# Storing the last tile's second sample by transfers of 5, 121 and 2 partitions

## The chip, the cores and the metric

The kernel runs on one core of a Trainium2 chip. A core has a matrix engine (TensorE, PE), a vector engine (VectorE, DVE), an activation engine (ScalarE, ACT), a general engine (GpSimd, POOL) and SyncE (SP), which here only issues transfers. Sixteen DMA engines move data between the on-chip memory (SBUF, 128 partitions) and the device memory (HBM). The metric is the device time of one execution in microseconds, and lower is better.

## The reference, cut to what matters

For 1024 samples, each with 39 fields of 16 numbers in `xi` and `xj`, every pair of fields (r, c) with c < r gives an outer product of 16 x 16. There are 741 pairs. Each pair is normalised over all samples and elements, scaled and shifted by `gamma` and `beta`, and multiplied by a 16 x 16 weight.

```python
cross = xj[:, rows, :, None] * xi[:, cols, None, :]          # (1024, 741, 16, 16)
mean = jnp.mean(cross, axis=(0, 2, 3), keepdims=True)
var = jnp.mean(jnp.square(cross - mean), axis=(0, 2, 3), keepdims=True)
normed = (cross - mean) * jax.lax.rsqrt(var + BN_EPS)
normed = normed * gamma[None, :, None, None] + beta[None, :, None, None]
out = normed[:, :, None, :, :] * W[None, None, :, :, :]
return jnp.transpose(out, (0, 2, 1, 3, 4))                   # (1024, 1, 741, 16, 16) float32
```

The output is 1024 x 741 x 256 float32 numbers, 777 million bytes; the inputs are about 6 million.

## The kernel before

Partition p holds samples 8p to 8p + 7 (`NT` = 8). The statistics come first, from sums of the inputs. Then the output is made tile by tile. A tile is one row r of the pair triangle for `T` = 2 samples of every partition, so it holds 128 x 2 x r pairs. The order of tiles ends with r = 21 and then r = 17, for the samples 6 and 7 of each partition.

```python
T = 2
...
tiles = [(mid, t0, t0 // T * half // 2) for t0 in range(0, NT, T)]      # mid = 19
slot = 0
for r in (mid + 1, *range(F - 1, mid + 1, -1)):
    for t0 in range(0, NT, T):
        tiles.append((r, t0, slot * half))
        if r < F - 1:
            tiles.append((F - 1 - r, t0, slot * half + T * r))
        slot ^= 1
...
out_v = out.rearrange("(p t) o n i j -> p t (o n i j)", t=NT)
```

ScalarE and GpSimd make the products of a tile, VectorE (with a share for GpSimd) adds the shift and multiplies by the weight, and the tile is stored from SBUF. All stores are issued by SyncE, in the order of the tiles. The function that issues them:

```python
def store(n, c0, c1, t_from=0, t_to=T):
    r, t0, _ = tiles[n]
    n0 = first[r]

    whole = n >= len(FIRST_PIECES)
    step = 1 if r > mid and (whole or c1 == r) else t_to - t_from
    for t in range(t_from, t_to, step):
        if whole and step == 1 and t == t_to - 1:
            if c1 < r:
                continue
            c0 = 0
        nc.sync.dma_start(
            out_v[:, t0 + t : t0 + t + step, (n0 + c0) * EE : (n0 + c1) * EE],
            view(n)[:, t : t + step, c0:c1, :].rearrange("p t n e -> p t (n e)"),
        )
```

For the last tile r = 17 is below `mid`, so `step` is 2: one transfer takes both samples of all 128 partitions. It is issued once the last of these has run:

```python
def finish(n):
    ...
    size = 1 if n == RAW else T
    for t in range(0, T, size):
        for c0, c1 in zip(bounds(n), bounds(n)[1:]):
            for c in [*range(c0, min(c1, p0)), *range(max(c0, p1), c1)]:
                stt(
                    y[:, t : t + size, c, :],
                    y[:, t : t + size, c, :],
                    t_sb[:, n0 + c : n0 + c + 1],
                    w_dve.to_broadcast([P, size, EE]),
                    ALU.add,
                    ALU.mult,
                )
            store(n, c0, c1, t, t + size)
```

Of the kernel before, what the change touches and what calls it, by code (L numbers as in the profile page):

```python
# [14 lines left out]
T = 2  # L15
# [25 lines left out]
def tile_pair_outer_batchnorm(  # L41
# [15 lines left out]
    nc = tc.nc  # L57
    P = nc.NUM_PARTITIONS
    NB, F, E = xi.shape
    NT = NB // P  # L60
    EE = E * E
# [7 lines left out]
    tiles = [(mid, t0, t0 // T * half // 2) for t0 in range(0, NT, T)]  # L69
# [25 lines left out]
    out_v = out.rearrange("(p t) o n i j -> p t (o n i j)", t=NT)  # L95
# [41 lines left out]
    def view(n):  # L137
        r, _, u = tiles[n]
        return y_sb[:, u : u + T * r, :].rearrange("p (t n) e -> p t n e", t=T)
# [65 lines left out]
    def store(n, c0, c1, t_from=0, t_to=T):  # L205
        r, t0, _ = tiles[n]
        n0 = first[r]

        whole = n >= len(FIRST_PIECES)
        step = 1 if r > mid and (whole or c1 == r) else t_to - t_from  # L210
# [9 lines that stand above are left out]
# [14 lines left out]
    def weigh(n):  # L234

        y = view(n)
        for c0, c1 in zip(bounds(n), bounds(n)[1:]):
            affine(n, range(c0, min(c1, OWN)), (nc.vector,))
            nc.vector.tensor_tensor(  # L239
                y[:, :, c0:c1, :],  # L240
                y[:, :, c0:c1, :],
                w_dve.unsqueeze(1).to_broadcast([P, T, c1 - c0, EE]),
                ALU.mult,
            )
            store(n, c0, c1)
# [8 lines left out]
    def finish(n):  # L254
# [33 lines left out]
# [12 lines that stand above are left out]
# [262 lines left out]
```

## Time and profile before

| what | value |
|---|---|
| time, median of 3 | 1879.16 us (1879.11 to 1879.3) |
| span of the profiled execution | 1877.4 us |
| written to HBM | 776.99 MB |
| rate over the span, read and written | 417 GB/s |
| transfers that store output | 279, all issued by SyncE |

The span is the time from the first to the last instruction in one profiled execution. The page divides it into 40 slices of 46.9 us each; the last store falls into the last slice alone, so what happens in it has to be asked for with narrower windows. A DMA share of 1 means that all 16 DMA engines move data; one engine is 0.06.

### The profile page before, as it was taken

To read this page: it belongs to the slowest core of one execution; us is meant where nothing else is said; L and a number is where in the kernel's file an instruction comes from. 1 tells how busy PE (TensorE), PEld (TensorE's weight loads), DVE (VectorE), ACT (ScalarE), POOL (GpSimd) and SP (SyncE) were. 2 spreads that over 40 slices of the span, in tenths; PEclk is the share of its full clock that TensorE was granted. 3 is DMA by queue.
4 is the path that set the end of the run, shared out by engine and by line. 5 is a ranking of instruction groups with operands and counts; after the bars stand their busy time and mean duration, and the time that the engine had idled before them with its cause. 6 is when DMAs were issued, how large, how long until landed. Compare 5 with 4: busy or idle time off the path is not lost.

```text
span 1877.4 us, 9638 instructions
## 1 busy us (share of the span) xinstructions
PE 26.0 (1%) x130; PEld 23.3 (1%) x130; DVE 1723.9 (92%) x2640; ACT 1645.7 (88%) x3416; POOL 1532.4 (82%) x1746
## 2 busy tenths in 40 slices
PE   4000000000000000000000000000000000000000
PEld 4000000000000000000000000000000000000000
DVE  8999888899999999999999999999999999999994
ACT  8999888888888899989999999998999998989892
POOL 8999778787777788888888888888888888888882
DMA  5999999999999999999999999999999999999998
GB/s 199 385 421 424 411 421 422 428 427 424 428 427 425 428 426 425 427 425 427 419 425 432 425 425 432 424 432 424 431 426 430 425 432 425 430 428 426 428 430 350
DMA packets 53690, 783.63 MB, mean 417 GB/s; under 512 B 4720, under 2 KB 6384, under 8 KB 17008
## 3 DMA queue, kind: packets, MB, share of 16 engines
q1 hardware_dynamic: 52320, 779.72, 97.9%
q10 hardware_dynamic: 1296, 3.29, 0.5%
q14 instruction: 73, 0.60, 0.1%
q8 instruction: 1, 0.02, 0.0%
HBM read 6.00 MB, written 776.99 MB: 417 GB/s over the span
## 4 chain that ended last, share of the span: by engine, by line
DMA 56%; ACT 21%; DVE 17%; issue 3%; POOL 1%; SPq 0%; ACTq 0%; DVEq 0%; PE 0%; POOLq 0%
DMA out_dram<-y_sb 56%; ACT y_sb L147 20%; DVE y_sb L291 16%; POOL y_sb L149 1%; DVE y_sb L358 1%; ACT y_sb L230 0%; DVE y_sb L332 0%; POOL xs L169 0%; SPq L216 0%; DMA xi_sb<-in_r_xi_dram 0%; POOL y_sb L277 0%; POOL y_sb L342 0%; DVE y_sb L192 0%; DVE xs L182 0%; ACT y_sb L353 0%
## 5 line engine op out<-in xcount | busy, mean ns | idle before, releaser
L291 DVE SCALAR_TENSOR_TENSOR y_sb<-y_sb,st_sb,w_dve 128x512 f32<-128x512 f32 (+1 forms) x2511 | 1653.2, 738 | 117.2 <-issue 103.9
L147 ACT ACTIVATE y_sb<-xs,xj_sb 128x288 f32<-128x288 f32 (+20 forms) x3194 | 1514.8, 565 | 181.5 <-DMA out_dram<-y_sb 149.6
L149 POOL TENSOR_SCALAR y_sb<-xs,xj_sb 128x480 f32<-128x480 f32 (+27 forms) x1126 | 604.8, 561 | 14.2 <-DMA out_dram<-y_sb 14.1
L280 POOL TENSOR_TENSOR y_sb<-y_sb,w_sb 128x2048 f32<-128x2048 f32 (+3 forms) x155 | 517.7, 3346 | 87.4 <-ACT y_sb L275 77.8
L169 POOL TENSOR_TENSOR xs<-xi_sb,st_sb 128x640 f32<-128x640 f32 (+33 forms) x135 | 183.9, 1363 | 199.9 <-ACT y_sb L147 196.1
L277 POOL TENSOR_SCALAR y_sb<-y_sb,st_sb 128x512 f32<-128x512 f32 x291 | 196.8, 692 | 5.1 <-ACT y_sb L147 5.1
L275 ACT ACTIVATE y_sb<-y_sb,st_sb 128x512 f32<-128x512 f32 x160 | 100.2, 708 | 3.8 <-POOL y_sb L149 2.2
L192 DVE TENSOR_TENSOR y_sb<-xs,ps 128x256 f32<-128x256 f32 (+3 forms) x32 | 24.8, 817 | 0.5
L489 PE MATMUL ps<-y_sb 39*128 39x38 f32 (+37 forms) x76 | 16.4, 397 | 2.8 <-DVE y_sb L475 2.8
L489 PEld LDWEIGHTS ps<-y_sb 39*128 39x128 f32 x76 | 16.3, 329 | 3.1 <-DVE y_sb L475 3.1
L353 ACT ACTIVATE y_sb<-y_sb 128x1248 f32<-128x1248 f32 x8 | 9.9, 1244 | 2.8 <-POOL y_sb L342 2.7
L358 DVE TENSOR_REDUCE y_sb<-y_sb 128x78 f32<-128x1248 f32 x8 | 11.2, 1445 | 0.4 <-ACT y_sb L353 0.4
L147 ACT ACTIVATE y_sb<-xi_sb,xj_sb 128x304 f32<-128x304 f32 x24 | 11.4, 537 | 0.0
L342 POOL TENSOR_TENSOR y_sb<-xi_sb,y_sb 128x1248 f32<-128x1248 f32 x4 | 9.2, 2322 | 2.2 <-ACT y_sb L391 2.2
L239 DVE TENSOR_TENSOR y_sb<-y_sb,w_dve 128x2048 f32<-128x2048 f32 (+4 forms) x6 | 10.7, 1838 | 0.1
L332 DVE TENSOR_REDUCE y_sb<-xi_sb 128x39 f32<-128x624 f32 (+1 forms) x6 | 6.1, 1011 | 3.9 <-DMA xi_sb<-in_r_xi_dram 3.9
L342 POOL TENSOR_TENSOR y_sb<-xj_sb,y_sb 128x1248 f32<-128x1248 f32 x4 | 9.2, 2318 | 0.0
L378 PE MATMUL ps<-y_sb 128*39 128x79 f32 x48 | 8.0, 340 | 15.2 <-DVE y_sb L358 15.1
L232 POOL TENSOR_SCALAR y_sb<-y_sb,st_sb 128x512 f32<-128x512 f32 x8 | 6.4, 812 | 2.2 <-ACT y_sb L147 2.2
L230 ACT ACTIVATE y_sb<-y_sb,st_sb 128x512 f32<-128x512 f32 x9 | 6.5, 803 | 0.2 <-ACT y_sb L147 0.2
L332 DVE TENSOR_REDUCE y_sb<-xj_sb 128x39 f32<-128x624 f32 (+1 forms) x6 | 6.1, 1014 | 0.5 <-DMA xj_sb<-in_r_xj_dram 0.5
L378 PEld LDWEIGHTS ps<-y_sb 128*39 128x39 f32 x48 | 5.8, 177 | 17.2 <-DVE y_sb L358 10.6
(59 smaller groups left out, 37.3 us busy)
## 6 DMA issues: line engine op xcount, KB each, us to landing
out_dram<-y_sb SPq DMA_DIRECT2D x25, 2304.0 KB, 10.4
out_dram<-y_sb SPq DMA_DIRECT2D x12, 3840.0 KB, 21.7
out_dram<-y_sb SPq DMA_DIRECT2D x21, 2048.0 KB, 12.4
out_dram<-y_sb SPq DMA_DIRECT2D x12, 3584.0 KB, 23.1
out_dram<-y_sb SPq DMA_DIRECT2D x12, 3328.0 KB, 24.4
out_dram<-y_sb SPq DMA_DIRECT2D x12, 3072.0 KB, 25.2
out_dram<-y_sb SPq DMA_DIRECT2D x16, 2176.0 KB, 11.0
out_dram<-y_sb SPq DMA_DIRECT2D x8, 4352.0 KB, 24.1
```

The lines of the kernel that those rows point to most:

```text
L147: nc.scalar.activation(y, src, AF.Copy, scale=scale)
L149: engine.tensor_scalar(y, src, scale, 1.0, ALU.mult, ALU.mult)
L169: nc.gpsimd.tensor_tensor(xs, xi_sb[:, t0 : t0 + T, 0:r, :], s_sb[:, :, n0 : n0 + r, :].to_broadcast([P, T, r, E]), ALU.mult,)
L192: nc.vector.tensor_tensor(view(n)[:, t].rearrange("p n (i j) -> p n i j", j=E), xs[:, t].unsqueeze(2).to_broadcast([P, r, E, E]), xj_short ...
L275: nc.scalar.activation(y[:, :, c, :], y[:, :, c, :], AF.Identity, bias=t_c)
L277: nc.gpsimd.tensor_scalar(y[:, :, c, :], y[:, :, c, :], t_c, 1.0, ALU.add, ALU.mult)
L280: nc.gpsimd.tensor_tensor(y[:, :, c0:c1, :], y[:, :, c0:c1, :], w_sb.unsqueeze(1).to_broadcast([P, T, c1 - c0, EE]), ALU.mult,)
L291: stt(y[:, t : t + size, c, :], y[:, t : t + size, c, :], t_sb[:, n0 + c : n0 + c + 1], w_dve.to_broadcast([P, size, EE]), ALU.add, ALU.mult,)
L342: nc.gpsimd.tensor_tensor(devs[n % 7], sources[x][:, t0 : t0 + T], shift[:, x : x + 1, :].unsqueeze(3).to_broadcast([P, T, F, E]), ALU.sub ...
L358: nc.vector.tensor_reduce(to[:, t0 : t0 + T, F : 2 * F], devs[n % 7], AX.X, ALU.add)
L378: nc.tensor.matmul(ps_g[acc][0:F, 0 : 2 * F + 1], lhs, fb[:, t], start=t == 0, stop=t == NT - 1)
L489: nc.tensor.matmul(ps[:, :, first[r] - n0 : first[r] - n0 + r], pick[:, r, :], stq[:, :, 0:r], start=True, stop=True,)
```

## The change

For the last tile alone, and only where both samples would be stored at once, the store is split. The first sample goes as one transfer of 128 partitions through SyncE's queue, as any other store. The second sample goes as three transfers: partitions 121 to 125 and then 0 to 120 through GpSimd's queue, and partitions 126 and 127 through SyncE's queue. The bytes are the same, and so is everything computed. The aim is to give the 16 DMA engines different amounts of the last data: [...]

```diff
     def store(n, c0, c1, t_from=0, t_to=T):
         r, t0, _ = tiles[n]
         n0 = first[r]
+        if n == len(tiles) - 1 and t_to - t_from == T:
+
+            store(n, c0, c1, 0, T - 1)
+            for engine, p0, p1 in ((nc.gpsimd, 121, 126), (nc.gpsimd, 0, 121), (nc.sync, 126, P)):
+                engine.dma_start(
+                    out_v[p0:p1, t0 + T - 1, (n0 + c0) * EE : (n0 + c1) * EE],
+                    view(n)[p0:p1, T - 1, c0:c1, :].rearrange("p n e -> p (n e)"),
+                )
+            return
 
         whole = n >= len(FIRST_PIECES)
         step = 1 if r > mid and (whole or c1 == r) else t_to - t_from
```

## The prediction

> **What bounds the kernel now.** I read the page's busy times first, then its slices and its list of DMA queues, and then asked the trace for the last 40 us, because only the last store is edited.
>
> ```profile
> PE 26.0 (1%) x130; PEld 23.3 (1%) x130; DVE 1723.9 (92%) x2640; ACT 1645.7 (88%) x3416; POOL 1532.4 (82%) x1746
> ...
> DMA  5999999999999999999999999999999999999998
> GB/s 199 385 421 424 411 421 422 428 427 424 428 427 425 428 426 425 427 425 427 419 425 432 425 425 432 424 432 424 431 426 430 425 432 425 430 428 426 428 430 350
> ...
> q1 hardware_dynamic: 52320, 779.72, 97.9%
> ...
> q14 instruction: 73, 0.60, 0.1%
> ```
>
> The 16 DMA engines are at 90% or more in every slice but the first and the last, at 411 to 432 GB/s. The 759 MB of output set the time and the compute engines run beside them. Two things matter for this change: the last slice is not full (350 GB/s), and a second queue, "instruction", moves 0.60 MB in 73 packets beside the stores.
>
> The timeline of the end shows when the last tile is finished and its one store issued:
>
> ```profile
> 1845.63 4.69 DVE L291 SCALAR_TENSOR_TENSOR y_sb<-y_sb,st_sb,w_dve 128x512 f32<-128x512 f32 x7
> 1850.47 0.38 SPq L216 DMA_DIRECT2D out_dram<-y_sb  x1
> ```
>
> The list of issues for the stretch from 1845 us gives that store's size and its time to landing:
>
> ```profile
> out_dram<-y_sb SPq DMA_DIRECT2D x1, 4352.0 KB, 26.0
> ```
>
> So computing is over at 1850.3, and 26 us pass until the store has landed, at about 1876.5. The chain of waits (SyncE's) ends on this: "SPq L557 <- DMA out_dram<-y_sb" holds 25.4 us in 4 waits. Nothing but DMA can shorten those 26 us. The table by stretches cuts them up (columns: stretch, its length, busy time of PE, PEld, DVE, ACT, POOL, clock, DMA share of the 16 engines, GB/s):
>
> ```profile
> 1850.50:1867.80 17.30, 0.00 (x0) 0.00 (x0) 0.00 (x0) 0.00 (x0) 0.00 (x0) 1.00 0.98 419
> 1868.20:1870.15 1.95, 0.00 (x0) 0.00 (x0) 0.00 (x0) 0.00 (x0) 0.00 (x0) 1.00 0.25 107
> 1870.15:1872.10 1.95, 0.00 (x0) 0.00 (x0) 0.00 (x0) 0.00 (x0) 0.00 (x0) 1.00 0.19 80
> 1872.10:1873.40 1.30, 0.00 (x0) 0.00 (x0) 0.00 (x0) 0.00 (x0) 0.00 (x0) 1.00 0.13 54
> 1873.40:1876.05 2.65, 0.00 (x0) 0.00 (x0) 0.00 (x0) 0.00 (x0) 0.00 (x0) 1.00 0.06 26
> 1876.05:1877.40 1.35, 0.00 (x0) 0.00 (x0) 0.00 (x0) 0.00 (x0) 0.00 (x0) 1.00 0.00 0
> ```
>
> The shares are 4, 3, 2 and 1 sixteenths (0.25, 0.19, 0.13, 0.06). Twelve engines run dry together at about 1868.1. Four go on: one to about 1870.15, one to 1872.1, one to 1873.4 and one to 1876.05. Then 1.35 us of program end. The slowest engine alone costs 7.95 us of the span.
>
> Why those four? Every store has 128 rows, 8 for each engine, so the stores are even. Their lags are 2.05, 4.0, 5.3 and 7.95 us, together 19.3. One engine moves 26 to 27 GB/s (107/4, 80/3, 26/1), so this is 19.3 x 27 = 0.52 MB. The instruction queue moves 0.60 MB (0.57 MB after the first 100 us). [...]
>
> [...]
>
> **The change part by part.** Bytes do not change. One row of one sample is 17 x 256 x 4 = 17,408 bytes, and 17,408 / 26.8 GB/s = 0.65 us of one engine.
> 1. Removed: the one transfer of 128 x 2 rows, 16 rows per engine. Added: a transfer of the first sample, 8 rows per engine, in SyncE's queue as before. It only shortens the packet list; no effect on the end.
> 2. The second sample, before 8 rows on each engine: now 1 row on five engines, 11 on eleven, and 2 more rows on the two lowest. A relieved engine does 7 rows less: 7 x 0.65 = 4.55 us. A loaded one does 3 more: 1.95 us. An engine with one of the two SyncE rows gains only 6 x 0.65 = 3.9 us.
> 3. Issue costs: two issues on GpSimd and one more on SyncE (0.38 us for the one shown). GpSimd ends its arithmetic at about 1844 and waits for VectorE until 1850.3; the engines have 17 us of queued work from there. [...]
> [...] Then the eleven end at 1868.1 + 1.95 = 1870.05. The four end at 1870.15, 1872.1, 1873.4 and 1876.05 minus 4.55: 1865.6, 1867.55, 1868.85, 1871.5; one on the two lowest engines ends 0.65 later. The last end is 1871.5, or 1872.15[...]. The gain is 4.55 or 3.9 us: 1879.16 - 4.55 = 1874.6, or 1875.3. I take the smaller gain[...].
>
> **Rivals.**
> - All 16 engines are used by the 121 rows[...]: fifteen engines keep 8 rows, five get 1 more, two another. The slowest engine then has 9 or 10 rows in place of 8: +0.65 to +1.3 us, so 1879.8 to 1880.5. Against it: the odd numbers 5 and 121 would be pointless. In the profile nothing decides.
> - [...] the slowest engine is one of the eleven and gets 3 more rows, +1.95 us: 1881.1. Again only the plan of the change speaks against it.
> - GpSimd's queue is slow to start or its rows are cut into small packets, so the eleven loaded engines end late. They have 1.5 us in hand (1870.05 against 1871.5), and 18 us until the queued work ends. A delay beyond that would eat the gain: 1877 to 1880.
> - A second lock on the end: if the program's end costs more with a third queue in use, a us or so is lost from the 1.35 us now seen after the last packet: 1876.
>
> **Range and chances.** Balanced perfectly, 19.3 us over 16 engines would leave the end at 1868.1 + 1.2 = 1869.3, a gain of 6.75 us (1872.4); no outcome is better than that by moving rows. I give the plan as drawn about two in three, [...] the rest to delays. So 1875.3, with 1873.8 to 1880.8 as the range. 2% is 38 us, and the change touches only the last 26, so same is nearly certain.
>
> **What would show it.** Right: in the profile after, a GpSimd queue with 126 data rows (2.19 MB) appears; the DMA share stays near 1 until about 1868, falls to 0.7 or so (eleven engines) until 1870, and then one engine or so lasts to 1871.5 or 1872.2; the instruction queue is unchanged; everything before 1850 is unchanged. Wrong: one engine still running past 1876, [...] or a gap in the DMA share between 1868 and the first GpSimd packets[...].

## The result, and the profile after

The changed kernel takes 1885.05 us (median of 6, 1884.51 to 1885.55) against 1879.06 us before (median of 6, 1878.91 to 1879.3). The ratio is 1.0032 with a 95% interval of 1.0019 to 1.0044. The prediction was 1875.3 us: a gain of 3.9 us was expected and a loss of 6.0 us was measured, above the top of the range (1880.8).

Up to the last store nothing differs: VectorE ends at 1850.07 us of the span, against 1850.32 before. The page of the changed kernel, slices and queues:

```profile
DMA  5999999999999999999999999999999999999997
GB/s 202 387 420 423 410 422 424 428 424 427 425 427 426 426 426 427 425 426 427 420 424 430 425 430 430 425 430 429 424 427 431 427 426 430 424 430 425 429 428 295
...
q1 hardware_dynamic: 52196, 777.53, 97.4%
q10 hardware_dynamic: 1296, 3.29, 0.5%
q0 software_dynamic: 176, 2.19, 0.4%
q14 instruction: 73, 0.60, 0.1%
```

Only the last slice is clearly different (295 GB/s in place of 350; no other differs by more than 7). Queue q0 is GpSimd's, with the 2.19 MB of 126 rows; the instruction queue still has 73 packets and 0.60 MB. The timeline has GpSimd's two issues at once after VectorE, so they are not late:

```profile
1850.73 1.28 POOL L212 DMA_DIRECT2D out_dram<-y_sb  x2 [6.75 <-DVE y_sb L300]
```

The table by stretches shows where the time went. Its columns are those of the table of before; the last two are the busy share of the 16 DMA engines and the rate.

```profile
1850.50:1867.80 17.30, 0.00 (x0) 0.00 (x0) 0.00 (x0) 0.00 (x0) 1.28 (x2) 1.00 1.01 335
1868.20:1870.15 1.95, 0.00 (x0) 0.00 (x0) 0.00 (x0) 0.00 (x0) 0.00 (x0) 1.00 0.80 265
1870.15:1872.10 1.95, 0.00 (x0) 0.00 (x0) 0.00 (x0) 0.00 (x0) 0.00 (x0) 1.00 0.71 258
1872.10:1873.40 1.30, 0.00 (x0) 0.00 (x0) 0.00 (x0) 0.00 (x0) 0.00 (x0) 1.00 0.48 188
1873.40:1876.05 2.65, 0.00 (x0) 0.00 (x0) 0.00 (x0) 0.00 (x0) 0.00 (x0) 1.00 0.33 134
1876.05:1882.25 6.20, 0.00 (x0) 0.00 (x0) 0.00 (x0) 0.00 (x0) 0.00 (x0) 1.00 0.10 42
```

In the first 17 us the engines are as busy as before (1.01 against 0.98) and move 335 GB/s in place of 419. So an engine that counts as busy need not be moving data at its full rate. The missing bytes are moved later, and the last packet ends at 1882.2 in place of 1876.05. The time after the last packet is 1.2 us (1.35 before). So the whole loss lies in the transfers themselves. The trace's packet records (start, duration and size of each DMA packet) say the same row by row: between 1855 and 1868 us a row of 17,408 bytes takes 0.97 us on average, and a third of them over 0.9 us; before it was 0.65 us and none.

### The profile page after: what moved, and what is told of

It reads as the page before. It is cut to its first block, busy times and chain, and to the rows that moved or that the text cites. A ratio compares the mean times of both kernels' runs of the same rounds, so it can differ in the third digit from the quotient of the medians.

```text
span 1883.4 us, 9644 instructions
## 1 busy us (share of the span) xinstructions
PE 26.0 (1%) x130; PEld 23.3 (1%) x130; DVE 1724.0 (92%) x2640; ACT 1645.8 (87%) x3416; POOL 1533.5 (81%) x1748
## 3 DMA queue, kind: packets, MB, share of 16 engines
q0 software_dynamic: 176, 2.19, 0.4%
## 4 chain that ended last, share of the span: by engine, by line
DMA 55%; ACT 21%; DVE 18%; issue 2%; POOL 1%; SPq 0%; ACTq 0%; DVEq 0%; PE 0%; POOLq 0%
DMA out_dram<-y_sb 55%; ACT y_sb L147 21%; DVE y_sb L300 17%; POOL y_sb L149 1%; DVE y_sb L367 1%; DMA xj_sb<-in_r_xj_dram 0%; POOL xs L169 0%; ACT y_sb L239 0%; DVE y_sb L341 0%; SPq L225 0%; DMA xi_sb<-in_r_xi_dram 0%; POOL y_sb L286 0%; DVE y_sb L192 0%; DVE xs L182 0%; ACTq L147 0%
## 6 DMA issues: line engine op xcount, KB each, us to landing
out_dram<-y_sb SPq DMA_DIRECT2D x25, 2304.0 KB, 10.4
```

## The experiments

Three causes were open. **Load**: the rows went to other engines than planned, and the slowest got more. **Queue**: packets of GpSimd's queue between those of SyncE's are slow in themselves. **Port**: the new transfers make an engine read partitions that another engine is reading at that time, and the two share one way out of SBUF. Where the text says "before", it is the kernel before run beside the experiment. The edits are shown in short form.

### One part at a time

The first kernel stores the second sample by GpSimd in one transfer of 128 partitions.

```diff
-for engine, p0, p1 in ((nc.gpsimd, 121, 126), (nc.gpsimd, 0, 121), (nc.sync, 126, P)):
+for engine, p0, p1 in ((nc.gpsimd, 0, P),):
```

> Second sample of the last tile stored by one 128-partition transfer through GpSimd's queue, first sample by SyncE as in the change. Port theory (the 5, 121 and 2 rows make DMA engines read partitions that other engines are reading too, and they slow one another): 128 rows are dealt out as all other stores are, so the rate stays near 420 GB/s until 1868 us and the time is that of before, 1879 to 1880. Queue theory (packets of GpSimd's queue beside SyncE's are slow in themselves): the dip in the rate stays, and the time is 1882 to 1886. Load theory (the rows went to the wrong engines, three more on the slowest): even rows again, 1879.

Measured: 1879.19 us, before 1879.08, ratio 1.0 (0.9991 to 1.0009). The same split without GpSimd:

```diff
+for engine, p0, p1 in ((nc.sync, 0, P),):
```

> Both samples stored by SyncE, one transfer of 128 partitions each: the change without its uneven rows and without GpSimd's queue. All theories: as before, 1878.8 to 1879.6. Anything else would mean that splitting the store costs by itself.

Measured: 1879.04 us, before 1879.08, ratio 0.9999 (0.9991 to 1.0008). Splitting the store costs nothing, as step 1 of the prediction had it.

The next leaves GpSimd out and keeps the rows per engine even, but in transfers that don't have 128 partitions.

```diff
+for engine, p0, p1 in ((nc.sync, 0, 112), (nc.sync, 112, P)):
```

> Second sample stored by SyncE alone, in transfers of 112 and of 16 partitions: 7 and 1 rows per engine if each uses 16 engines, so as many rows per engine as before, but not the partitions that the engine otherwise reads. Port theory: a dip in the rate and packets over 1 us, time 1881 to 1886. Queue theory and load theory: 1879 to 1879.5, since nothing goes through GpSimd and the rows are even.

Measured: 1881.65 us, before 1879.08, ratio 1.0014 (1.0007 to 1.0021): 2.6 us lost without GpSimd and without uneven rows. And the change with its two GpSimd transfers exchanged:

```diff
+for engine, p0, p1 in ((nc.gpsimd, 0, 121), (nc.gpsimd, 121, 126), (nc.sync, 126, P)):
```

> The change with its two GpSimd transfers in the other order, 121 rows first and then 5: [...] each transfer reads the partitions of the change. Load theory: which engines are relieved is what matters, so the time moves by several us, to 1874 to 1876 if the slowest engines are now relieved, or stays at 1885 with another engine last. Port theory: a dip in the rate and an end later than before in any case, 1881 to 1888. Queue theory: within 1 us of the change, 1885.

Measured: 1885.53 us, before 1879.08, ratio 1.0033 (1.002 to 1.0046). The order makes no difference that can be seen. Port and queue fit this, and load isn't excluded by it, since its expectation also allowed 1885 us with another engine last.

The stretch from 1855 to 1868 us sets the four apart. First the whole second sample by GpSimd, which keeps the rate of before:

```profile
1855.00:1868.00 13.00, 0.00 (x0) 0.00 (x0) 0.00 (x0) 0.00 (x0) 0.00 (x0) 1.00 1.00 425
```

Then 112 and 16 rows by SyncE:

```profile
1855.00:1868.00 13.00, 0.00 (x0) 0.00 (x0) 0.00 (x0) 0.00 (x0) 0.00 (x0) 1.00 1.03 387
1868.00:1876.05 8.05, 0.00 (x0) 0.00 (x0) 0.00 (x0) 0.00 (x0) 0.00 (x0) 1.00 0.37 112
```

And the change in the other order:

```profile
1855.00:1868.00 13.00, 0.00 (x0) 0.00 (x0) 0.00 (x0) 0.00 (x0) 0.00 (x0) 1.00 1.00 298
```

The kernel before and the change itself, in this order:

```profile
1855.00:1868.00 13.00, 0.00 (x0) 0.00 (x0) 0.00 (x0) 0.00 (x0) 0.00 (x0) 1.00 0.99 425
1855.00:1868.00 13.00, 0.00 (x0) 0.00 (x0) 0.00 (x0) 0.00 (x0) 0.00 (x0) 1.00 1.00 302
```

The queue theory falls with the first, which has 144 packets in GpSimd's queue and no dip. The dip comes with the partition counts.

### Where the slow engines are

```diff
+# after each of tiles len-16 .. len-2, with k = 1, 2, ... 15
+nc.sync.dma_start(spare[0:k, 0:4352], xi_rows[0:k, 0:4352])    # HBM to HBM
```

> A probe, on the kernel before: beside the stores of fifteen of the last sixteen tiles SyncE issues copies from HBM to HBM of 1, 2, ... 15 rows of 17,408 bytes, so that the lowest-numbered DMA engine gets 15 rows more and the highest none, if k rows go to the lowest k engines. The sixteen engines should then run dry at the end in a stair of about 0.65 us a step, with four of them late by 2.4, 4.4, 5.6 and 8 us against their step. If the four that lag are the lowest five, as the prediction took it, the lowest steps are those missing, and the last end is 15 us or more after the first. If they lie elsewhere, the missing steps say where. Not a version to use: it copies rows nobody needs.

By the packet records the engines ended at 1869.07, 1870.12, 1870.64, 1871.16, 1871.62, 1872.12, 1872.68, 1873.25, 1873.89, 1874.55 and 1875.16 us, and then at 1877.65, 1879.49, 1880.68, 1883.32 and 1883.61. That is a stair of eleven ends, 0.5 to 0.7 us apart (the first step is 1.05), and five ends that don't fit it. Five more steps of 0.57, about the mean of the last nine, would have lain at 1875.73 to 1878.01, with the sum 9384.35; with the four lags of the kernel before, read here from its packet records (2.39, 4.38, 5.64 and 8.02, together 20.43), that gives 9404.78. The five measured ends sum to 9404.75. So the four slow engines are among the five that got most rows, and this premise held. These are the lowest five: the even steps fit k rows that go to the first k engines of one fixed order. From the first end to the last it is 14.5 us, a little under the 15 expected. Which of the five lags by how much isn't shown.

### What an engine loses at a shared port

At the end of the kernel before, once its stores have landed, rows of 34,816 bytes are stored one transfer at a time:

```diff
+for rows in (slice(0, 1), slice(0, 4), slice(0, 16, 4), slice(0, 128, 32)):
+    nc.vector.memset(last, 0.0)            # waits until the transfer before has landed
+    nc.sync.dma_start(spare[rows], last[rows])
```

> A probe at the end of the kernel before, when all other transfers have landed: SyncE stores rows of 34,816 bytes from SBUF to spare HBM, one transfer at a time: first partition 0 alone, then 0 to 3, then 0, 4, 8, 12, then 0, 32, 64, 96. One row takes one engine 1.3 us, and the four rows of a transfer go to four engines. Port theory[...]: 0, 4, 8, 12 land as fast as one row; 0 to 3 lie on one port and take 3 x 1.3 = 3.9 us longer; 0, 32, 64, 96 lie on two ports and take 1.3 us longer. Without a shared port all four land alike.

The stretches from the first packet to the end of the last, in that order:

```profile
1886.48:1887.78 1.30, 0.00 (x0) 0.00 (x0) 0.00 (x0) 0.00 (x0) 0.00 (x0) 1.00 0.06 27
1898.09:1903.56 5.47, 0.00 (x0) 0.00 (x0) 0.00 (x0) 0.00 (x0) 0.00 (x0) 1.00 0.24 25
1914.49:1915.86 1.37, 0.00 (x0) 0.00 (x0) 0.00 (x0) 0.00 (x0) 0.00 (x0) 1.00 0.24 102
1926.60:1929.35 2.75, 0.00 (x0) 0.00 (x0) 0.00 (x0) 0.00 (x0) 0.00 (x0) 1.00 0.24 51
```

One engine with one row moves 27 GB/s. Four engines that read partitions 0 to 3 move 25 GB/s together, and each of their packets takes 5.1 to 5.2 us in place of 1.29. Partitions 0, 4, 8, 12 let the four run at full rate (1.29 us each), and 0, 32, 64, 96 at half (2.6 to 2.7 us). All four engines count as busy each time: the share is 0.24 at 25, 102 and 51 GB/s. So partitions 0 to 3 behave as if they shared one port of about one engine's rate (25 GB/s), 0, 4, 8 and 12 as if they shared none, and 0, 32, 64 and 96 as if two and two shared one (51 GB/s, twice 25.5). Which two go together isn't shown, and no other partitions were tried here.

### How the rows are dealt out

Again at the end of the kernel before, one transfer at a time, rows of 17,408 bytes:

```diff
+alone(nc.gpsimd, slice(0, 121))      # SBUF to spare HBM
+alone(nc.sync,   slice(0, 121))
+alone(nc.gpsimd, slice(121, 126))
+alone(nc.gpsimd, slice(0, 128, 12))  # 11 rows
+extra(nc.gpsimd, 0, 121)             # HBM to HBM
```

> A probe at the end of the kernel before, when its stores have landed; one transfer at a time, rows of 17,408 bytes (0.65 us of one engine), all from SBUF but the last: GpSimd 121 rows, SyncE 121 rows, GpSimd 5 rows, GpSimd 11 rows twelve partitions apart, GpSimd 121 rows from HBM to HBM. If GpSimd's 121 rows go to 11 engines, as predicted, 11 packets start at once and the last transfer takes 11 x 0.65 = 7.2 us; if to 16 engines[...], 16 start at once and 8 follow each other, 5.2 us. Port theory: SyncE's and GpSimd's 121 rows from SBUF take longer than that, with packets above 1 us, and the 11 rows, on eleven ports, take 0.65 us each; the 5 rows, on two ports, 1.3 to 2 us.

From first packet to last end, in that order:

```profile
1878.43:1888.84 10.41, 0.00 (x0) 0.00 (x0) 0.00 (x0) 0.00 (x0) 0.00 (x0) 1.00 0.87 202
1890.18:1902.96 12.78, 0.00 (x0) 0.00 (x0) 0.00 (x0) 0.00 (x0) 0.00 (x0) 1.00 0.59 165
1904.96:1907.02 2.06, 0.00 (x0) 0.00 (x0) 0.00 (x0) 0.00 (x0) 0.00 (x0) 1.00 0.24 42
1908.90:1909.66 0.76, 0.00 (x0) 0.00 (x0) 0.00 (x0) 0.00 (x0) 0.00 (x0) 1.00 0.61 252
1911.37:1918.33 6.96, 0.00 (x0) 0.00 (x0) 0.00 (x0) 0.00 (x0) 0.00 (x0) 1.00 0.90 303
```

GpSimd's 121 rows start as 16 packets at once and go on as 15: fifteen engines with 8 rows and one with 1. SyncE's 121 rows start as 11. So GpSimd deals these rows out as the first rival had it, and the 11 engines of the prediction are what SyncE uses. GpSimd's eight rows per engine should take 5.2 us (8 x 0.65) and take 10.4; a packet takes mostly 1.3 us, twice the row's time. If each engine takes eight neighbouring partitions, as I suppose, sixteen engines start on partitions 0, 8, 16, ... at once, among them 0, 32, 64 and 96, which ran at half rate in the probe before: the same factor of two. That the other starts pair up in the same way wasn't measured. The eleven rows twelve partitions apart take 0.65 us each, and the five neighbouring rows 1.1 to 2.0 us. From HBM to HBM the same 121 rows take 7.0 us, 0.82 us a row on average. That is less than from SBUF and still more than 5.2, so not all of the excess in this probe can be put down to SBUF's ports; what the rest is stays open.

The second probe adds the change's three transfers to the whole kernel before, but as copies from HBM to HBM.

```diff
+extra(nc.gpsimd, 121, 126); extra(nc.gpsimd, 0, 121); extra(nc.sync, 126, P)    # after the last store
```

> A probe, on the kernel before: its store is left whole, and transfers of 5 and 121 rows by GpSimd and of 2 rows by SyncE are added that copy rows of 17,408 bytes from HBM to HBM, so that SBUF is not read by them. Port theory: packets keep about 0.65 us, no stretch with a share of 1 and 300 GB/s. If packets are stretched here too, the slowing isn't SBUF's. The loads should show, at 1 row for five engines and 11 for eleven: eleven engines end 7.2 us later, at 1875.3. If the slowest engine is one of the five, it ends at 1876.7 to 1877.4 and the span hardly grows; if it is one of the eleven, at 1883.2. If all 16 engines share the 121 rows, 8 each, at 1881.3.

```profile
1855.00:1868.00 13.00, 0.00 (x0) 0.00 (x0) 0.00 (x0) 0.00 (x0) 0.00 (x0) 1.00 0.98 417
```

GpSimd's rows ran from 1849 to 1863.5 us (6 us earlier than in the change, since they need not wait for VectorE), took 0.67 us on average (median 0.648), and the rate stayed at 417 GB/s. The last packet ended at 1881.7: 5.7 us after the 1876.05 of before, which is 8 to 9 rows on the slowest engine (5.2 to 5.85 us), close to what was expected for sixteen engines (1881.3). With SBUF left out, the same two queues and row counts do no harm but their own work.

### How much each part costs

```diff
+for engine, p0, p1 in ((nc.gpsimd, 0, 121), (nc.sync, 121, P)):
```

> The change without its 5-row transfer: 121 rows of the second sample by GpSimd, the other 7 (121 to 127) by SyncE. If the 121 rows carry the loss (sixteen engines, eight rows each[...]; 10.4 us alone in place of 5.2), the rate still dips to about 300 GB/s and the time is 1883 to 1885.5. If the few rows at the lowest engines and at the last two ports carry it, the time is below 1882.

Measured: 1884.53 us, before 1879.45, ratio 1.0026 (1.0017 to 1.0036), 5.1 us.

```diff
+# kernel before, its store whole, and after it, into spare HBM
+for engine, p0, p1 in ((nc.gpsimd, 121, 126), (nc.sync, 126, P)):
+    engine.dma_start(spare[p0:p1, 0:ROW], last[p0:p1, ROW : 2 * ROW])
```

> The kernel before with its store left whole, and seven rows stored once more, from SBUF to spare HBM: partitions 121 to 125 by GpSimd and 126, 127 by SyncE, as in the change. It does more work than the change in these rows and none of the 121. If the 121 rows carry the loss, this costs the added rows on the slowest engine and some sharing of two ports: 0.6 to 2 us, 1879.7 to 1881. If the small transfers carry it, 3 us or more, 1882 or later.

Measured: 1881.05 us, before 1879.45, ratio 1.0009 (1.0 to 1.0017), 1.6 us. The table by stretches for each, the 121 rows without the 5 first, and then the 5 and 2 rows added to the kernel before:

```profile
1855.00:1868.00 13.00, 0.00 (x0) 0.00 (x0) 0.00 (x0) 0.00 (x0) 0.00 (x0) 1.00 1.00 299
```

```profile
1855.00:1868.00 13.00, 0.00 (x0) 0.00 (x0) 0.00 (x0) 0.00 (x0) 0.00 (x0) 1.00 0.99 402
```

The 121 rows carry most of the loss. The few rows cost 1.6 us in a kernel that stores them twice, with an interval that begins at no loss. Their trace shows sharing too: GpSimd's five rows took 2.2 us on average, up to 3.4. The two sum to 6.7 us against 6.0 of the change, a difference that lies within the intervals.

### Can the plan be carried out at all?

The last pair tried to do what the change was drawn for: none of the second sample on the lowest five engines. GpSimd stores groups of 11 and 10 partitions, twelve apart (11 such rows alone took 0.65 us each), and small copies between them are meant to move its starting engine past the lowest five. That the starting engine moves with the rows of the transfer before was assumed; no run had shown it. First as additional copies in HBM:

```diff
+turn(5)                                    # 5 rows of 512 bytes, HBM to HBM
+for j in range(12):
+    nc.gpsimd.dma_start(spare_j[j:P:12, 0:ROW], xi_rows[j:P:12, 0:ROW])
+    turn(5 if j < 8 else 6)
+turn(11)
```

> A probe, on the kernel before: GpSimd adds HBM to HBM copies of 8 x 11 and 4 x 10 rows of 17,408 bytes, and between them copies of 5 or 6 rows of 512 bytes, [...] each large copy should begin at the engine after the lowest five. SBUF is not read by them. [...] the lowest five engines get nothing but the small rows and end as before, the last at 1876 to 1876.5, and ten engines end 12 x 0.5 to 0.65 us later, at 1874 to 1876. If the rows start at engine 0 each time, the slowest engines get up to 12 rows more and the last end is at 1882 to 1884.

The time was 1888.93 us (before 1879.27). By the packet records SyncE's rows on the four slow engines ended at 1877.2, 1879.9, 1881.2 and 1883.2 us, 6.8 to 7.5 us later than before. The slow engines did get rows: at 0.65 us each the delay is about eleven of them, nearly one from each of the twelve copies. Whether the starting engine is another than assumed when the kernel starts, or doesn't move as assumed, this run doesn't tell. The same with the output itself:

```diff
+    nc.gpsimd.dma_start(out_v[j:P:12, ...], view(n)[j:P:12, T - 1, c0:c1, :]...)
```

> What the change was for, done in a way that should really relieve the lowest five engines, and on the change's own split: the second sample goes by GpSimd in 8 transfers of 11 and 4 of 10 partitions, twelve partitions apart and so on different ports, with small HBM copies of no use between them[...]. The lowest five engines get no row of this sample, ten get 12. Load theory (only the engine's work counts): the slowest engine has 8 rows less, the last end is near 1871, and the time 1874. Port theory ([...] each port moves one engine's rate): no gain, 1879 or more, likely 1881 to 1886 for the collisions.

Measured: 1886.25 us, before 1879.27, ratio 1.0037 (1.0021 to 1.0053). It doesn't decide between load and port, since its premise failed, and since GpSimd waited for its own transfers between issues. From the chain of waits of GpSimd near the end:

```profile
POOL out_dram L229 <- DMA out_dram<-y_sb: 13.4, 5, 5.3
```

Its last issues came at 1880 us. One thing it does show: eleven such rows alone took 0.65 us each, but here, beside the stores of 128 partitions, GpSimd's rows took 0.89 us on average between 1855 and 1868 us. Whether real relief would help stays open.

## Why the prediction was wrong, point by point

- **What bounds the end** was read rightly: four DMA engines run late. That they are among those that the change was to relieve was a guess; the stair puts them among the lowest five. Why they are late was not shown. The prediction had 0.52 MB for the lags and 0.57 MB in the instruction queue, and the 69 packets of that queue after the first 100 us took 21.5 us together, close to the 20.43 us of the four lags; that fits but doesn't show which engine moved them.
- **Step 1**, no cost for splitting the store, held (ratio 0.9999).
- **Step 3**, no cost for issuing, held: GpSimd issued at 1850.73 us and its first rows moved at about 1855, with work queued on the engines all the while; 128 rows by GpSimd cost nothing (ratio 1.0).
- **Step 2 failed twice.** It put "1 row on five engines, 11 on eleven", a split that no trace of before showed. In the probe GpSimd's 121 rows went to sixteen engines, 8 on fifteen of them, so the relief of 7 rows (4.55 us) never existed, and a slow engine that gets one of the 5 or 2 rows has more to do. This was the first rival, to which the prediction gave 1879.8 to 1880.5, and which it set aside because the odd numbers 5 and 121 "would be pointless". The intention of a change is no evidence of what it does.
- The second failure has no rival in the prediction: it took a row to cost 0.65 us on whichever engine moves it. That held in the kernel before, where every store has 128 partitions (0.65 us on average). With 121 rows the mean row took 0.97 us while they were in flight, and the end came 6.15 us later. The 121 rows explain 5.1 us of it in their own run. Most of that must be sharing: their row count adds nothing to fifteen engines, and SyncE's 7 rows there at most one row each; in isolation the 121 took 10.4 us in place of 5.2.
- **Rows and sharing can be told apart in the trace of the change.** Each packet of a DMA engine starts within 5 ns of the end of its last, so the latest engines' packets can be strung together although the records don't name the engine. Which engine of before each one is can be told from the packets of the earlier stores on it, whose times are 0.25 to 0.3 us earlier in this run; between the late engines these times differ by more than 1 us. The engine that was last before, at 1876.04, moved 8 of the 121 rows and one of the five, one row more than before, and ended at 1878.05. The last end, 1882.22, is that of the engine that had ended at 1873.67. It moved two rows more than before (1.3 us). Its row of the five took 3.54 us, its eight of the 121 took 7.97 in place of 5.2, and four of SyncE's rows between them took 1.9 us more than usual. By rows alone the last end would have been at about 1876.7 (an estimate: 1876.04 and one row), so about 5.5 of the 6.15 us are sharing.
- **What would show it wrong** named "one engine still running past 1876", which is what is seen (four of them do, with a share of 0.10 until 1882.25), but it would have been read as a slow engine that was not relieved. The sign that tells the causes apart is the rate at full share, 335 GB/s at 1.01, and the prediction didn't name it.
- **The range** ended at 1880.8 because its bad outcomes were counted in rows, and it left out one of them, the 1881.1 of the second rival. In these runs rows moved work about, and sharing took rate away (302 GB/s in place of 425 from 1855 to 1868 us).
- **Readings that were off**, none of which changes the step that failed: the output is 777 MB and not 759; the second slice has 385 GB/s and so lies outside "411 to 432"; and the lags of 2.05, 4.0, 5.3 and 7.95 us, read from windows, are 2.39, 4.38, 5.64 and 8.02 us by the packet records.

## What to carry to other kernels

Transfers of all 128 partitions kept 420 to 425 GB/s beside one another from 1855 to 1868 us, from either queue. With the other partition counts tried here (121 with 5 and 2: 302 GB/s; 121 with 7: 299; 112 with 16: 387), from either queue, engines made one another wait, so an uneven split has to be judged by which partitions are read at the same time as well as by rows per engine. A busy share of DMA need not say anything about rate: read the share and the GB/s together. Here a stretch at share 1.00 and 302 GB/s in place of 425 was contention. And how a transfer is dealt out over the engines should be measured by itself, on idle queues, before a plan is built on it: one probe showed 16 packets starting where 11 were assumed.

## What the runs showed that was not expected

- Four engines that read neighbouring partitions 0 to 3 move 25 GB/s together, what one engine moves alone (27 GB/s), and all four are shown as busy.
- GpSimd and SyncE deal out the same 121 rows differently: fifteen engines with 8 rows and one with 1 in 10.4 us, against 11 engines in 12.8 us; by rows alone it would be 5.2 and 7.2 us.
- Queued behind other stores, GpSimd's 128 rows lost nothing by being in a second queue: 425 GB/s with 144 of its packets in it.
